# Layer 0's keys turned by a product with a diagonal matrix instead of a scaling and a transpose, and the last table load placed behind two copies

## The chip, the cores and the metric

The kernel runs on one core of a Trainium2 chip. The core has a matrix engine (TensorE, "PE" in the profile, with its weight loads listed apart as "PEld"), a vector engine (VectorE, "DVE"), an engine for functions by table (ScalarE, "ACT"), a general engine (GpSimd, "POOL") and a queue engine that issues the DMA transfers (SyncE, "SP"). Each engine works through its own list of instructions in order and waits at an instruction until what it needs is there. The metric is the device time of one execution in microseconds (us); lower is better.

## The reference

Two layers, each a cross attention and a feed-forward part with residuals. The change touches the cross attention of layer 0 alone, on 32 batches of 64 tokens of width 512:

```python
features_n = rmsnorm(features, fn_w)
Q = einsum('btd,fd->btf', text, Wq_w) + Wq_b        # text: layer norm of x
K = einsum('bsd,fd->bsf', features_n, Wk_w) + Wk_b
Q = rmsnorm(Q, qn_w)
K = rmsnorm(K, kn_w)
scores = einsum('btf,bsf->bts', Q, K) / sqrt(512)
x = x + einsum('bts,bsf->btf', softmax(scores), features_n)
...                                                 # layer 0's ffn, layer 1's attention and ffn
```

All of it is in 32-bit floats.

## The kernel before

The 2048 token rows are 16 tiles of 128 rows. Layer 0's attention goes through them in eight passes of two tiles, `for i in range(NP)` with i from 0 to 7. A pass holds four batches of 64 tokens.

In pass i, `keys_of` turns the normed tokens (`pt`, four 128x128 transposes for each tile, L181), multiplies the context by the key weights (`pk`, L374), and lets VectorE take each product out of PSUM into `kb`, one row for each key, scaled by the context's own norm and with the bias added (L377). ScalarE sums the squares of `kb` into `sq` (L381). `queries_of` makes the queries in the same way (`pq`, L397; `qb`, L398; squares, L400), turns them (`ptq`, L181) and copies them to `qT` (L405). `norm_of` turns the sums of squares into one over the root mean square, by a square root on ScalarE (L356) and a reciprocal on VectorE (L357).

The keys of pass i are turned one pass later, in pass i+1, by `turn_keys`: VectorE scales the rows of `kb` in place by `sq` (L415, one instruction for each of two tiles), TensorE transposes the scaled rows (`ptk`, eight transposes, L181 through the helper `transposed`), and VectorE takes the result out of PSUM with the norm weights multiplied in (`kT`, L420). TensorE then adds the values of the pass before (`po`, L471) and makes the scores (`psc`, L432, 16 products of 64x64). The last pass has no successor: it turns its own keys too, inside `queries_of` through `between()`.

The softmax takes the largest score (L437), multiplies it with the queries' scale (L439; in the last pass L441, which also multiplies by `one`), and takes the exponential on ScalarE (L445). ScalarE needs another table for the exponential than for the square root, and each change of table is an `ACT_TABLE_LOAD`. In the last pass a one-element exponential that gives the number 1 (`one`, L409) makes the table load happen before the scores are there; L441 reads `one`, and so waits for it.

The framework puts the instructions of every engine into an order before the kernel runs; `tc.issue_after(x)` puts what is inside behind x, and a tile from a pool waits until the buffer's last user is done. On TensorE the order of a later pass is `pt` x8, `pk` x8, `pa_t` (turned softmax weights), `ptk` x8, `po` x4, `psc` x16, `pq` x8, `ptq` x8, with some steps of layer 0's feed-forward part between them. GpSimd meanwhile makes sums of weights (L127) and products for the feed-forward part's choice (L272), which are started behind the normed context `cn` (L451). SyncE issues tokens (L314), context (L320, L325), and weights for the feed-forward part (L516, L522, L610).

One matrix product in 32-bit floats shows in the trace as two records of TensorE, a transpose as one.

Of the kernel before, what the change touches and what calls it, by code (L numbers as in the profile page):

```python
# [8 lines left out]
F32 = mybir.dt.float32  # L9
I32 = mybir.dt.int32  # L10
BF16 = mybir.dt.bfloat16
AF = mybir.ActivationFunctionType
ALU = mybir.AluOpType
# [3 lines left out]
P = 128  # L17
# [3 lines left out]
C = D // P  # L21
# [14 lines left out]
def tile_kernel(  # L36
# [25 lines left out]
    nc = tc.nc  # L62
# [5 lines left out]
    ident = const.tile([P, P], F32, name="ident")  # L68
# [110 lines left out]
    def transposed(ps, src):  # L179
        for c in range(C):  # L180
            nc.tensor.transpose(ps[:, c, :], src[:, c * P : (c + 1) * P], ident)  # L181


    with ExitStack() as l0:
# [108 lines left out]
        with ExitStack() as pa:  # L293
            wpool = pa.enter_context(tc.tile_pool(name="l0w", bufs=1))
            wk = pa.enter_context(tc.tile_pool(name="l0work", bufs=2))
# [11 lines left out]
            one = wpool.tile([P, 1], F32, name="one")  # L307
# [47 lines left out]
            def norm_of(sq):  # L355
                nc.scalar.activation(sq, sq, AF.Sqrt, bias=eps6, scale=1.0 / D)  # L356
                nc.vector.reciprocal(sq, sq)  # L357

            def keys_of(i, ct, xn, rs):

                kb = wk.tile([P, 2, D], F32, name=f"kb_{i}", tag="kb")
                sq = small.tile([P, 4], F32, name="sq4", tag="sq4")
                xT = wk.tile([P, 2, C, P], F32, name="xT", tag="xT", bufs=1)
                for tt in range(2):
                    pt = ps_t.tile([P, C, P], F32, name="pt", tag="pt")
                    transposed(pt, xn[:, tt, :])
                    turned = nc.scalar.copy(xT[:, tt], pt)
                if i == 0:
                    with tc.issue_after(turned.ins):
                        norm_context(cn[0], rs[:, 2:4])  # L370
                for tt in range(2):
                    pk = ps_m.tile([P, D], F32, name="pk", tag="pm")
                    for c in range(C):
                        nc.tensor.matmul(  # L374
                            pk, ct[:, c, tt * P : (tt + 1) * P], WK[:, c, :], start=c == 0, stop=c == C - 1
                        )
                    nc.vector.scalar_tensor_tensor(  # L377
                        kb[:, tt, :], pk, rs[:, 2 + tt : 3 + tt], bk, ALU.mult, ALU.add
                    )
                    scr = wk.tile([P, D], F32, name="scr", tag="scr", bufs=1)  # L380
                    nc.scalar.activation(scr, kb[:, tt, :], AF.Square, accum_out=sq[:, 2 + tt : 3 + tt])  # L381
                return kb, sq, xT

            def queries_of(i, xT, sq, between):

                qT = wk.tile([P, 2, C, P], F32, name=f"qT_{i}", tag="qT")
                qb = wk.tile([P, 2, D], F32, name="qb", tag="qb", bufs=1)
                last = i == NP - 1
                if last:
                    norm_of(sq[:, 2:4])  # L390

                    with tc.issue_after(exped[-1]):
                        nc.scalar.activation(one, eps6, AF.Sqrt)
                for tt in range(2):
                    pq = ps_m.tile([P, D], F32, name="pq", tag="pm")
                    for c in range(C):
                        nc.tensor.matmul(pq, xT[:, tt, c, :], WQ[:, c, :], start=c == 0, stop=c == C - 1)  # L397
                    query_added.append(nc.vector.tensor_add(qb[:, tt, :], pq, bq).ins)  # L398
                    scr = wk.tile([P, D], F32, name="scr", tag="scr", bufs=1)
                    nc.scalar.activation(scr, qb[:, tt, :], AF.Square, accum_out=sq[:, tt : tt + 1])  # L400
                between()
                for tt in range(2):
                    pt = ps_t.tile([P, C, P], F32, name="ptq", tag="pt")
                    transposed(pt, qb[:, tt, :])
                    nc.scalar.copy(qT[:, tt], pt)  # L405
                norm_of(sq[:, 0:2] if last else sq)
                if last:

                    nc.scalar.activation(one, sq[:, 0:1], AF.Exp, scale=0.0)  # L409
                return qT  # L410

            def turn_keys(kb, sq):
                kT = [wk.tile([P, C, P], F32, name="kT", tag="kT") for _ in range(2)]
                for tt in range(2):
                    nc.vector.tensor_scalar(  # L415
                        kb[:, tt, :], kb[:, tt, :], sq[:, 2 + tt : 3 + tt], None, ALU.mult
                    )
                    pt = ps_t.tile([P, C, P], F32, name="ptk", tag="pt")
                    transposed(pt, kb[:, tt, :])
                    nc.vector.tensor_mul(kT[tt], pt, wqk[:, :, None].to_broadcast([P, C, P]))  # L420
                return kT

# [168 lines left out]
            for i in range(NP):  # L591
# [27 lines left out]
                kb, sq, xT = keys_of(i, ct.pop(i), xn, rs)  # L619
                if i == 0:  # L620
                    ready = norm(1, cn[1])
                if i:
                    rs1, kb1, sq1, qT = keys.pop(i - 1)
                    add = turn_and_add(i - 2) if i > 1 else lambda: None
                    kT = turn_keys(kb1, sq1)
                    add()
                    *scored[i - 1], (_, _, normed) = scores(cn[i - 1], rs1, qT, sq1, kT)
                    with started_behind(normed):
                        sum_up()
                        for n in range(*{3: (0, 2), 4: (2, 4), 5: (4, 6), 6: (6, 7), 7: (7, 8)}.get(i, (0, 0))):  # L630
                            w = [t[:, :, QW * (n // 4) : QW * (n // 4) + QW] for t in W1]
                            four_sums(nc.gpsimd, w[4:], *w[:4], False, (n % 4,))
                place(i, 1)

                def between():
                    if i == NP - 1:
                        add = turn_and_add(i - 1)
                        last.append(turn_keys(kb, sq))
                        add()

                qT = queries_of(i, xT, sq, between)
                keys[i] = (rs, kb, sq, qT)
                place(i, 2)
# [12 lines left out]
        with ExitStack() as pb:  # L656
            wk = pb.enter_context(tc.tile_pool(name="ffnwork", bufs=2, reuse_waits="tile"))
# [180 lines left out]
    with ExitStack() as pc:  # L838
# [3 lines left out]
        wk = pc.enter_context(tc.tile_pool(name="l1work", bufs=2, reuse_waits="tile"))  # L842
# [123 lines left out]
        def project_q(xts, g, T):  # L966

            w = load_weights(q_quarter, WQS, g, T, False, "wq", 7)
            qT = wk.tile([P, 8, J, S], F32, name="qT1", tag="qT1", bufs=1)
            qsq = wk.tile([P, 8, J, S], F32, name="qsq", tag="qsq", bufs=1)  # L970

            def mm(i, ps, first):
                last = products(
                    ps, lambda h, c: w[i][:, c, h * HD : (h + 1) * HD],
                    lambda h, c: xts[RIGHT[i]][:, c, :], first,
                )
                projected.append(last.ins)
                if T == 0:
                    keep_sum(w, i, WQS, g, False, last)

            def quarter(t, hh, th):
                return t[:, 4 * th : 4 * th + 4, 2 * hh : 2 * hh + 2, :].rearrange("p b j t -> p j b t")

            def put(hh, th, ps, kept):
                o = quarter(qT, hh, th)
                ps = ps.rearrange("p j (b t) -> p j b t", t=S)
                if kept is None:
                    keeps.append(nc.scalar.copy(o, ps).ins)
                else:
                    ins = nc.vector.tensor_add(o, ps, kept.rearrange("p j (b t) -> p j b t", t=S))  # L990
                    puts.append(ins.ins)
                o = qT[:, 4 * th : 4 * th + 4, 2 * hh : 2 * hh + 2, :]
                nc.scalar.activation(  # L993
                    qsq[:, 4 * th : 4 * th + 4, 2 * hh : 2 * hh + 2, :], o, AF.Square
                )

            winograd(bank, mm, sbuf_keep, put)
            return qT, qsq
# [228 lines left out]
        qT, qsq = project_q(xts, 0, 0)  # L1227
# [12 lines left out]
        for n, (T, g) in enumerate(units):  # L1240
# [14 lines left out]
            if more:  # L1255
# [9 lines left out]
                qT, qsq = project_q(xts, g2, T2)  # L1265
# [223 lines left out]
```

## Time and profile before

| | |
|---|---|
| three runs | 1830.59, 1834.60, 1836.09 us; median 1834.6 us |
| the profiled execution | 1834.12 us, span 1832.3 us |
| granted TensorE clock | 0.997 of full speed, mean |
| busy in the span: PE, DVE, ACT, POOL | 1807.5, 945.5, 655.2, 733.7 us |
| layer 0's attention | the first 179.6 us of the span |
| in it: `ptk` transposes | 64 records on TensorE |
| in it: scaling of `kb` (L415) | 16 instructions on VectorE, 13.4 us |

A row of the groups reads: line, engine, operation, output and inputs by the program's names, shapes, count; then busy time in us and the mean of one in ns; then the engine's idle time just before and what ended it. A row of a timeline reads: start in us, us, engine, line, operation, count, and in brackets the idle time before it with what ended it. Where several equal instructions follow each other, a timeline merges them; the start of the next row is then a better end than start plus length, since TensorE's matmuls overlap at their ends. The chain of waits is followed back from the last instruction and is given here in order of time.

### The profile page before, as it was taken

The page shows a single profiled execution, that of the slowest core. Times are in us where ns is not written, and L with a number is a line of the kernel's source. Part 1 is how long each engine was busy: PE and PEld are TensorE (multiplying, and loading weights), DVE is VectorE, ACT ScalarE, POOL GpSimd, SP SyncE. Part 2 cuts the span into 40 slices and gives each one's busy share as a digit, 9 for nine tenths or more (in the row PEclk, how much of TensorE's full clock was granted, in tenths as well). Part 3 has the DMA queues.
Part 4 walks back from the last instruction along what each step waited for, and adds up shares of the span by engine and source line. Part 5 has one row for each costly group of instructions (what it writes and reads, how often), then busy time and mean ns, then how long its engine had stood idle before and what let it go on. Part 6 is the DMA issues. An engine that isn't in the chain of part 4 may idle for free.

```text
span 1832.3 us, 29495 instructions
## 1 busy us (share of the span) xinstructions
PE 1807.5 (99%) x11620; PEld 1472.1 (80%) x11620; DVE 945.5 (52%) x1665; ACT 655.2 (36%) x1187; POOL 733.7 (40%) x630
## 2 busy tenths in 40 slices
PE   8999999999999999999999999999999999999998
PEld 4545989888998888888888888888888888888764
DVE  5887555655425444445444445444444554544466
ACT  4544322222113433434343334333342434434411
POOL 1542444344337575654422344324242342222422
PEclk9999999999999999999999999999999999999999
DMA  9632300000024434544444354443454334443413
GB/s 252 183 116 89 128 22 22 21 22 22 22 69 146 148 117 157 183 158 127 137 128 128 114 150 122 130 129 112 130 154 130 118 119 132 139 133 102 160 40 93
DMA packets 157210, 210.89 MB, mean 115 GB/s; under 512 B 14928, under 2 KB 95824, under 8 KB 156432
## 3 DMA queue, kind: packets, MB, share of 16 engines
q1 hardware_dynamic: 155712, 206.91, 37.1%
q8 instruction: 92, 1.51, 0.3%
q10 hardware_dynamic: 1360, 2.10, 0.3%
q14 instruction: 46, 0.38, 0.1%
HBM read 176.74 MB, written 32.21 MB: 114 GB/s over the span
## 4 chain that ended last, share of the span: by engine, by line
PE 93%; DVE 2%; ACT 2%; POOL 1%; DMA 1%; issue 1%; SPq 0%; POOLq 0%; ACTq 0%; DVEq 0%
PE b L901 51%; PE ph L727 10%; PE po L770 9%; PE sc L1065 3%; PE pv L1124 3%; PE pq L397 3%; PE pd L1334 2%; PE pk L374 2%; PE pr L1037 2%; PE pta L1106 2%; PE pt L181 1%; PE pi L279 1%; PE ptk L1023 1%; DVE x L1413 0%; PE psc L432 0%
## 5 line engine op out<-in xcount | busy, mean ns | idle before, releaser
L1154 DVE TENSOR_TENSOR x<-x,b 128x512 f32<-128x512 f32 x224 | 153.8, 687 | 208.4 <-PE b L901 208.4
L901 PE MATMUL b<-tx,wq 128*128 128x256 f32 x1024 | 243.2, 383 | 2.8 <-POOL tx L127 1.4
L901 PE MATMUL b<-wo,so 128*128 128x256 f32 x1024 | 232.5, 380 | 3.8 <-issue 3.8
L127 POOL TENSOR_TENSOR so<-oT 128x512 f32<-128x512 f32 x64 | 81.0, 1287 | 359.1 <-ACT oT L1130 359.1
L901 PEld LDWEIGHTS b<-tx,wq 128*128 128x128 f32 x1024 | 191.0, 190 | 40.4 <-ACT keep L909 7.7
L901 PEld LDWEIGHTS b<-wo,so 128*128 128x128 f32 x1024 | 194.7, 190 | 30.9 <-issue 4.4
L901 PE MATMUL b<-xt,wq 128*128 128x256 f32 x768 | 186.2, 381 | 0.0
L901 PE MATMUL b<-wo,oT 128*128 128x256 f32 x768 | 184.9, 381 | 0.0
L1089 POOL TENSOR_TENSOR prob<-prob,mx 128x512 f32<-128x512 f32 x64 | 67.9, 1063 | 247.4 <-DVE mx L1088 129.5
L901 PEld LDWEIGHTS b<-wo,oT 128*128 128x128 f32 x768 | 145.6, 191 | 20.3 <-issue 1.0
L901 PEld LDWEIGHTS b<-xt,wq 128*128 128x128 f32 x768 | 143.1, 190 | 19.1
L1110 ACT COPY aT<-pta 128x512 f32<-128x512 f32 x64 | 34.5, 589 | 303.2 <-PE pta L1106 303.2
L909 ACT COPY keep<-b 128x512 f32<-128x512 f32 x144 | 82.4, 582 | 136.7 <-PE b L901 136.7
L901 PE MATMUL b<-wkv,sc 128*128 128x256 f32 x512 | 115.7, 379 | 0.0
L993 ACT ACTIVATE qsq<-qT 128x512 f32<-128x512 f32 x128 | 80.3, 628 | 88.9 <-DVE qT L990 88.2
L901 PEld LDWEIGHTS b<-wkv,sc 128*128 128x128 f32 x512 | 97.2, 190 | 13.2
L272 POOL TENSOR_TENSOR e<-e,down 128x896 f32<-128x896 f32 (+1 forms) x40 | 68.2, 1711 | 90.4 <-DVE e L268 88.8
L1077 DVE TENSOR_REDUCE mx<-prob 128x8 f32<-128x512 f32 x64 | 43.9, 686 | 116.7 <-POOL prob L1072 116.7
L770 PE MATMUL po<-w,gT 128*128 128x256 f32 x448 | 101.9, 382 | 0.0
L770 PEld LDWEIGHTS po<-w,gT 128*128 128x128 f32 x448 | 84.0, 190 | 18.7 <-issue 7.8
L990 DVE TENSOR_TENSOR qT<-b,keep 128x512 f32<-128x512 f32 x96 | 65.6, 686 | 57.4 <-PE b L901 57.4
L901 PE MATMUL b<-wkv,ct 128*128 128x256 f32 x384 | 94.8, 383 | 0.0
(213 smaller groups left out, 3142.4 us busy)
## 6 DMA issues: line engine op xcount, KB each, us to landing
wq<-in_wq SPq DMA_DIRECT2D x104, 256.0 KB
wo<-in_wo SPq DMA_DIRECT2D x104, 256.0 KB
wq<-wqs SPq DMA_DIRECT2D x96, 256.0 KB
wo<-wos SPq DMA_DIRECT2D x96, 256.0 KB
wkv<-in_wkv SPq DMA_DIRECT2D x52, 256.0 KB
wkv<-wks SPq DMA_DIRECT2D x48, 256.0 KB
wqs<-wq SPq DMA_DIRECT2D x32, 256.0 KB
wos<-wo SPq DMA_DIRECT2D x32, 256.0 KB
```

What stands on the lines that cost most here:

```text
L127: ins = eng.tensor_tensor(s[k], *pairs[k], op)
L272: nc.gpsimd.tensor_tensor(e3, e3, down[:, None, :].to_broadcast([P, k, BLK]), ALU.mult)
L397: nc.tensor.matmul(pq, xT[:, tt, c, :], WQ[:, c, :], start=c == 0, stop=c == C - 1)
L727: nc.tensor.matmul(ps[:, c, :], W1[LEFT[i]][:, d, (c0 + c) * P : (c0 + c + 1) * P], xq[RIGHT[i]][:, d, :], start=first and c == 0 and d == ...
L770: nc.tensor.matmul(ps, chunk(gq[LEFT[i]], c), W2[RIGHT[i]][:, c, :], start=first and c == 0, stop=c == HC - 1, skip_group_check=True,)
L901: last = nc.tensor.matmul(out[:, h, :], lhs(h, c), rhs(h, c), start=first and h == 0 and c == 0, stop=c == 1, skip_group_check=True,)
L909: keeps.append(nc.scalar.copy(e, ps).ins)
L990: ins = nc.vector.tensor_add(o, ps, kept.rearrange("p j (b t) -> p j b t", t=S))
L993: nc.scalar.activation(qsq[:, 4 * th : 4 * th + 4, 2 * hh : 2 * hh + 2, :], o, AF.Square)
L1065: score = nc.tensor.matmul(sc[k * S : (k + 1) * S, 4 * a + 2 * pp + b, :], qT[:, at, 2 * pp + k, :], kT[:, bb * S : (bb + 1) * S], start=T ...
L1089: ins = nc.gpsimd.tensor_tensor(pr, pr, mx[:, 1, :, None].to_broadcast([P, 8, S]), ALU.mult)
L1154: added.append(nc.vector.tensor_add(xq[:, i, j], xq[:, i, j], ps).ins)
```

## The change

`turn_keys` no longer scales the key rows. VectorE makes, for each tile, a 128x128 matrix `diag` that is the unit matrix with row p multiplied by the key's factor (L418 in the new file), and TensorE multiplies the unscaled rows by it: four ordinary products of 128x128 with `diag` as the moving operand in place of four transposes with the unit matrix. The result in PSUM is the same turned and scaled block. In the last pass, the one-element exponential with its table load is put behind the second copy of `qT`.

```diff
                 for tt in range(2):
                     pt = ps_t.tile([P, C, P], F32, name="ptq", tag="pt")
                     transposed(pt, qb[:, tt, :])
-                    nc.scalar.copy(qT[:, tt], pt)
+                    copied = nc.scalar.copy(qT[:, tt], pt)
                 norm_of(sq[:, 0:2] if last else sq)
                 if last:
-                    nc.scalar.activation(one, sq[:, 0:1], AF.Exp, scale=0.0)
+                    with tc.issue_after(copied.ins):
+                        nc.scalar.activation(one, sq[:, 0:1], AF.Exp, scale=0.0)
                 return qT

             def turn_keys(kb, sq):
                 kT = [wk.tile([P, C, P], F32, name="kT", tag="kT") for _ in range(2)]
                 for tt in range(2):
-                    nc.vector.tensor_scalar(
-                        kb[:, tt, :], kb[:, tt, :], sq[:, 2 + tt : 3 + tt], None, ALU.mult
-                    )
+                    diag = wk.tile([P, P], F32, name="diag", tag="diag", bufs=2)
+                    nc.vector.tensor_scalar(diag, ident, sq[:, 2 + tt : 3 + tt], None, ALU.mult)
                     pt = ps_t.tile([P, C, P], F32, name="ptk", tag="pt")
-                    transposed(pt, kb[:, tt, :])
+                    for c in range(C):
+                        nc.tensor.matmul(
+                            pt[:, c, :], kb[:, tt, c * P : (c + 1) * P], diag, start=True, stop=True
+                        )
                     nc.vector.tensor_mul(kT[tt], pt, wqk[:, :, None].to_broadcast([P, C, P]))
                 return kT
```

In the order of the instructions, TensorE's and GpSimd's lists stay as they are but for the products. On ScalarE the table load and `one` change places with the two copies. On VectorE a few neighbours change places: in pass 1 one scaling of the context (L451) comes ahead of the two `kT`, and the second normed token tile ahead of `qb`; in pass 5 one normed token tile ahead of `kb`. On SyncE, in pass 2, a token load moves ahead of the turned context, one load of the feed-forward weights (L610) ahead of the context load (L320) and four stores (L522), and another ahead of the load of L516.

## The prediction

> **What bounds it now.** I read the page first: TensorE is busy nearly all the time, and its list keeps its order under the change. A delay of TensorE in layer 0 therefore moves all that follows, and time is won only where TensorE stands idle. (PEld overlaps PE.)
>
> ```profile
> PE 1807.5 (99%) x11620; PEld 1472.1 (80%) x11620; DVE 945.5 (52%) x1665; ACT 655.2 (36%) x1187; POOL 733.7 (40%) x630
> ```
>
> Then the groups of the first 200 us, shapes apart, for the prices and for the idle time around the operations touched:
>
> ```profile
> L181 PE MATMUL ptk<-ident,kb 128*128 128x128 f32 x64 | 8.3, 273 | 0.0
> L432 PE MATMUL psc<-kT,qT 128*64 128x64 f32 x256 | 9.2, 225 | 3.6 <-DVE kT L420 2.5 <-ACT qT L405 0.9
> ...
> L415 DVE TENSOR_SCALAR kb<-kb,sq 128x512 f32<-128x512 f32 x16 | 13.4, 857 | 0.1
> L498 DVE TENSOR_SCALAR wqk<-wqk 128x4 f32<-128x4 f32 x1 | 0.2, 170 | 0.0
> ```
>
> TensorE never idles ahead of `ptk`; it idles behind it, ahead of `psc`. The scaling by VectorE costs no time by itself, only through `kT`. The listed idle time between 20 and 180 us is 1.61 + 0.91 + 0.52 + 0.89 + 0.74 + 0.35 = 5.0 us; that is all that can be won there at full clock.
>
> The chain of waits in pass 3 gives the rate of a transpose and the usual course behind it:
>
> ```profile
> 71.26 0.87 PE ptk L181 x8
> 72.13 1.02 PE po L471 x8
> 73.15 0.04 issue
> 73.19 1.15 PE psc L432 x32
> ```
>
> Eight transposes take 0.87 us, 109 ns each. An ordinary 32-bit product with the same operand shapes is `ph` of the feed-forward part, in TensorE's timeline at full clock:
>
> ```profile
> 185.51 2.84 PE L727 MATMUL ph<-xT,w 128*128 128x128 f32 x24
> 188.19 1.50 PE L727 MATMUL ph<-xT,w1s 128*128 128x128 f32 x12
> ```
>
> 24 records in 188.19 - 185.51 = 2.68 us are 111.7 ns each, and a product is two records: 223 ns.
>
> Last, two stretches of the timeline where TensorE does wait, pass 2 and the end of pass 7:
>
> ```profile
> 45.03 2.71 DVE L415 TENSOR_SCALAR kb<-kb,sq 128x512 f32<-128x512 f32 x2
> 45.09 2.37 POOL L127 TENSOR_TENSOR w1s<-w,w 128x896 f32<-128x896 f32 x1 [1.31 <-DVE sq L357]
> ...
> 48.52 3.30 DVE L451 SCALAR_TENSOR_TENSOR cn<-cn,rs,fnb 128x512 f32<-128x512 f32 x2
> 48.53 2.08 POOL L127 TENSOR_TENSOR w1s<-w1s,w 128x896 f32<-128x896 f32 x1 [1.07 <-DMA w<-in_w]
> ...
> 53.73 1.15 PE L432 MATMUL psc<-kT,qT 128*64 128x64 f32 x32 [1.61 <-DVE kT L420]
> ```
>
> ```profile
> 171.89 1.28 ACT L409 ACT_TABLE_LOAD   x1
> ...
> 173.19 0.20 ACT L409 ACTIVATE one<-sq 128x1 f32<-128x1 f32 x1
> 173.29 1.06 ACT L405 COPY qT<-ptq 128x512 f32<-128x512 f32 x2
> 173.91 1.17 PE L432 MATMUL psc<-kT,qT 128*64 128x64 f32 x32 [0.89 <-ACT qT L405]
> ...
> 175.53 0.22 DVE L441 SCALAR_TENSOR_TENSOR nm<-nm,one,sq 128x2 f32<-128x2 f32 x1
> 175.84 0.41 ACT L445 ACTIVATE s<-psc,nm,sq 128x64 f32<-128x64 f32 x1 [1.50 <-DVE nm L441]
> ```
>
> In pass 2, VectorE's second scaling ends 0.25 us after GpSimd's sum, and its first `cn` 2.1 us late: the two stop each other. At the end, the table load stands between `sq` and the copies, and `psc` waits for the copies.
>
> **The products.** Eight passes of eight: 8 x (223 - 109) ns = +0.92 us of TensorE a pass, 7.3 us in all. Off the path VectorE loses 16 scalings and gains 16 of a quarter the size. No row shows that size; the bounds are 0.17 us (L498, 4 elements) and 0.47 us (L415 unhindered, at 30.61 us). I take 0.25, by length between them. The dispute with GpSimd stays, so only what VectorE itself works is surely saved.
>
> A rule speaks against this: the Trainium skill, Perfetto Trace Analysis, section Transposes, says that a logical transpose should be a transpose and not a standard matmul, since it skips the arithmetic. TensorE: Matmul & The Clock Gate, Terms, puts the transpose mode at four times faster for FP32, which would make the eight products 3.48 us and the added TensorE time 8 x 2.61 = 20.9 us. The rows' factor is 2.05, and the sum goes by the rows.
>
> Pass by pass, as delay of `psc` against before:
>
> - Pass 1. Between `ptk` and `psc` lie 1.72 us of `pq`, which cover the two `kT` (1.26 us) and the `cn` put ahead of them (0.72 us; without that cover 2.0 us more). +0.92.
> - Pass 2. Unhindered, `psc` would have stood at 53.73 - 1.61 = 52.12; with two passes' products TensorE gets there at about 53.9. On VectorE the second sum of GpSimd, which a DMA starts and not TensorE, again holds `cn` until 50.6, then `kb` to 52.5 and `kT` (behind the second half of `ptk` at 53.0) to 53.8. So `psc` starts at about 53.83: the delay falls to 0.10, this pass gives -0.82. If GpSimd's sums move along with TensorE, it gives up to +0.9.
> - Passes 3, 4, 6, 7. `po` alone takes 1.02 us (170.91 to 171.93), yet `psc` follows it after 1.13: 0.11 us is a wait for `kT`. `ptk` ends 0.92 later, `kT` is ready at 73.72 in pass 3, `po` ends at 74.0, and `po` becomes the later one. 4 x (0.92 - 0.11) = +3.24.
> - Pass 5. `psc` at 118.55 comes 0.94 us after `po` could be done; VectorE has been busy without a break since 106.5. Both L415 there (0.86 and 1.08 us) shrink, the second by less because GpSimd's product runs beside it: 0.4 to 1.5 us saved. The products fill the gap: -0.02, up to +0.5.
> - The end. `ptk` +0.92 puts `ptq` at 172.85; its first copy starts 0.63 us later, as at 41.34 and 41.97, so 173.48, and `psc` at 174.10. The copies end at 174.57, the load takes 1.28 and `one` 0.2: 176.09. L441 waits for it and starts at 176.13, not 175.53. So the load leaves the copies' way and enters L441's: +0.60. Without the products the same move would give -0.36, since the copies could have begun 0.73 us earlier and then `one`, not `psc`, would be last. The exponential L445, `pa_t` and all of layer 1 queue behind L441's wait.
>
> On SyncE the two weight loads (448 KB each) pass the context load and four stores. At the 243 GB/s of the stretch from 40 to 60 us one of them takes 1.9 us; the context, issued at 52.20, is read first at 64.33 with no wait for a DMA. The load of L516 was waiting for the stores anyway. Nothing; without that cover 1.9 us.
>
> Sum: 0.92 - 0.82 + 3.24 - 0.02 + 0.60 = +3.9 us. The profiled execution of 1834.1 would become 1838.0; the median lies 0.5 above it, so 1838.5.
>
> **Rivals.** (a) The gaps aren't filled: VectorE stays behind GpSimd, passes 2 and 5 give +0.92 each. Then 2 x 0.92 + 3.24 + 0.92 + 0.60 = +6.6: 1841.2. For it speaks the long wait in pass 2; against it that the sum there follows a DMA. (b) The granted clock: a view of the windows has 1.00 up to 176, 0.63 from 176 to 178, 0.50 to 182, 0.66 to 184. `po` then takes 2.08 and not 1.02 us, the first 12 `ph` 2.72 and not 1.34, the next 24 3.17 and not 2.68: 2.9 us. If the drop fails to come, the sum is +1.0: 1835.6. If the longer idle ahead of `pa_t` (0.74 becomes 1.1) adds another, +6.8: 1841.4. The runs before spread over 5.5 us, so both are possible. (c) Faster: the product with `diag` costs one record, 112 ns. Then passes 3, 4, 6, 7 and pass 2 stay, pass 5 gives -0.94 and the end -0.36: -1.3, 1833.3. It would decide below 143 ns a product, where 6 x (added TensorE time of a pass) equals 1.64 us (the gap of pass 5, four waits of 0.11, the end's 0.36, less pass 2's 0.10). Against it: every ordinary 32-bit product of this trace has two records. (d) The move of the load brings nothing because L441 reads `one`: it is in my sum.
>
> **Numbers.** Forecast 0.50, (a) 0.24, (b) no drop 0.12, (b) another drop 0.07, (c) 0.05; 0.02 left for a product far dearer than two records. The range reaches from (c) past (a) and (b): 1833.0 to 1843.0. A measurement of this kernel tells 0.3%, 5.5 us, from no change: 1829.1 to 1840.1. Slower by more are (a) with 0.20 of its 0.24, the second drop with 0.06, 0.04 of the forecast's upper end and the 0.02: 0.32. Faster by more needs (c) with no drop: 0.02. Within: 0.66.
>
> **What would show it.** Right: `ptk` with 128 records at 112 ns; `psc` in passes 3, 4, 6, 7 right behind `po`; no wait, or a short one, ahead of `psc` in passes 2 and 5; L441 right behind `one`; layer 0's end 3 to 5 us later at equal clock. Wrong: `ptk` in 0.9 us; a wait for `kT` of over 1 us in pass 2; a `psc` of the last pass that starts before 173.9; another count of half-clock stretches.

## The result and the profile after

| | before | after |
|---|---|---|
| median of ten runs | 1833.47 us | 1837.6 us |
| lowest, highest | 1830.59, 1836.09 us | 1836.16, 1840.69 us |
| the profiled execution: time, span | 1834.12, 1832.3 us | 1837.26, 1835.5 us |
| mean granted clock in it | 0.997 | 0.998 |

The ratio of the times is 1.0024, with a 95% interval of 1.0015 to 1.0032: the changed kernel is 4.4 us slower (2.8 to 5.9). The medians differ by 4.1 us, which is 0.23%. From L424 on, a line of the changed file is 4 higher than the line of the same step before (`psc` L432 is L436, `po` L471 is L475, `kT` L420 is L424, L441 is L445).

The engines' line of the changed kernel's page has 64 matmul records more on TensorE, and nearly 7 us more of its busy time:

```profile
PE 1814.4 (99%) x11684; PEld 1479.5 (81%) x11684; DVE 943.2 (51%) x1665; ACT 654.8 (36%) x1187; POOL 733.2 (40%) x630
```

The groups of the first 204 us, TensorE's rows. A row's mean counts overlapping ends; for a rate, starts are compared further down.

```profile
L421 PE MATMUL ptk<-diag,kb 128*128 128x128 f32 x128 | 15.6, 275 | 0.0
...
L436 PE MATMUL psc<-kT,qT 128*64 128x64 f32 x256 | 9.2, 225 | 0.2 <-ACT qT L405 0.2
```

The turned keys are now 128 records, and the scores' idle time has gone from 3.6 to 0.2 us; the wait for `kT` has left the row. Between 20 and 183 us, all that TensorE still waits for is this (engine, line, what was waited for; us in total, times, longest us):

```profile
PE pa_t L463 <- ACT s L449: 1.1, 1, 1.1
PE pt L181 <- ACT qT L405: 0.5, 1, 0.5
PE po L475 <- ACT aT L465: 0.4, 1, 0.4
PE psc L436 <- ACT qT L405: 0.2, 1, 0.2
```

That is 2.2 us, none of it for a DMA; the kernel before waited 5.0 us in the same view. So TensorE waits less and is later all the same. TensorE's timeline in pass 3 shows a pass where nothing waits:

```profile
71.51 1.95 PE L421 MATMUL ptk<-diag,kb 128*128 128x128 f32 x16
73.39 1.09 PE L475 MATMUL po<-cn,aT 64*64 64x512 f32 x8
74.41 1.15 PE L436 MATMUL psc<-kT,qT 128*64 128x64 f32 x32
```

From `ptk` to `po` it is 73.39 - 71.51 = 1.88 us, against 0.97 in the same view of before (71.09 to 72.06), so the products add 0.91 us. And `psc` stands 1.02 us behind the start of `po`, just the time of `po`; before it stood 1.13 us behind.

In pass 2 (all engines) the 1.61 us ahead of `psc` are gone:

```profile
45.74 2.08 POOL L127 TENSOR_TENSOR w1s<-w,w 128x896 f32<-128x896 f32 x1 [0.16 <-DMA w<-in_w]
...
46.22 1.88 DVE L418 TENSOR_SCALAR diag<-ident,sq 128x128 f32<-128x128 f32 x2
...
49.06 1.42 DVE L455 SCALAR_TENSOR_TENSOR cn<-cn,rs,fnb 128x512 f32<-128x512 f32 x2
...
50.08 2.35 POOL L127 TENSOR_TENSOR w1s<-w1s,w 128x896 f32<-128x896 f32 x1 [2.26 <-DMA w<-in_w]
...
53.13 1.09 PE L475 MATMUL po<-cn,aT 64*64 64x512 f32 x8
53.23 0.69 DVE L424 TENSOR_TENSOR kT<-ptk,wqk 128x512 f32<-128x512 f32 x1 [0.20 <-PE ptk L421]
54.15 1.15 PE L436 MATMUL psc<-kT,qT 128*64 128x64 f32 x32
```

VectorE waits for TensorE here (the second `kT` for `ptk`), and `psc` follows `po`. The first of the two `diag` steps is held by GpSimd's first sum, though it is a quarter of the size; the pair ends 0.28 us behind it, as the two scalings did before. The two `cn` took 3.30 us before and take 1.42 now, because GpSimd's second sum, which waits for a DMA, began at 50.08 and not at 48.53.

At the end of the attention the table load has left the copies' way and stands ahead of L445:

```profile
177.32 1.07 ACT L405 COPY qT<-ptq 128x512 f32<-128x512 f32 x2 [1.66 <-PE ptq L181]
...
177.96 1.17 PE L436 MATMUL psc<-kT,qT 128*64 128x64 f32 x32 [0.24 <-ACT qT L405]
...
178.41 1.28 ACT L410 ACT_TABLE_LOAD   x1
...
179.70 0.20 ACT L410 ACTIVATE one<-sq 128x1 f32<-128x1 f32 x1
179.94 0.22 DVE L445 SCALAR_TENSOR_TENSOR nm<-nm,one,sq 128x2 f32<-128x2 f32 x1 [0.47 <-ACT one L410]
...
181.19 0.33 PE L463 MATMUL pa_t<-ident,s 128*128 128x128 f32 x1 [1.11 <-ACT s L449]
```

The wait ahead of `psc` is 0.24 and not 0.89 us, the one ahead of `pa_t` 1.11 and not 0.74.

The last reading is the clock. The windows view has, behind the stretch and its length, the busy time of each engine, then PEclk, DMA share and GB/s. First the kernel before, then the changed one:

```profile
176.00:177.00 1.00, 0.26 (x3) 0.18 (x1) 0.86 (x3) 0.73 (x4) 0.00 (x0) 0.77 0.45 131
177.00:178.00 1.00, 0.65 (x5) 0.39 (x8) 0.98 (x2) 0.27 (x1) 0.41 (x1) 0.50 0.58 162
...
183.00:184.00 1.00, 1.00 (x9) 1.00 (x9) 0.00 (x0) 0.07 (x1) 0.00 (x0) 0.82 1.08 444
```

```profile
181.00:182.00 1.00, 0.46 (x2) 0.27 (x4) 1.00 (x4) 0.40 (x3) 0.00 (x0) 0.97 0.88 97
182.00:183.00 1.00, 1.00 (x8) 0.30 (x8) 0.39 (x1) 0.00 (x0) 1.00 (x1) 0.50 0.55 159
...
185.00:186.00 1.00, 1.00 (x9) 1.00 (x9) 1.00 (x2) 0.00 (x0) 0.00 (x0) 0.82 1.08 370
```

All windows left out are at 0.50. Counted as time at half clock, before has 0.46 + 6 + 0.36 = 6.8 us, after has 0.06 + 3 + 0.36 = 3.4 us. So the two profiled executions do not stand on the same clock, and the spans' difference of 3.2 us has to be taken apart. The first `pt` comes 0.28 us later; from there to the last `pa_t` the changed kernel loses 4.13 us at full clock; from `pa_t` to the first `ph` it wins 0.12; and the first 36 records of `ph` take 2.12 + 2.68 us and not 2.72 + 3.17, which wins 1.09. 0.28 + 4.13 - 0.12 - 1.09 = 3.20 us, the whole of 1835.5 - 1832.3. Nothing of the difference lies behind layer 0's attention but this clock.

### The profile page after: what moved, and what is told of

The parts are those of the page before. It is cut to its first block, busy times and chain, and to the rows that moved or that the text cites. A ratio compares the mean times of both kernels' runs of the same rounds, so it can differ in the third digit from the quotient of the medians.

```text
span 1835.5 us, 29626 instructions
## 1 busy us (share of the span) xinstructions
PE 1814.4 (99%) x11684; PEld 1479.5 (81%) x11684; DVE 943.2 (51%) x1665; ACT 654.8 (36%) x1187; POOL 733.2 (40%) x630
## 4 chain that ended last, share of the span: by engine, by line
PE 95%; ACT 2%; DVE 1%; POOL 0%; issue 0%; DMA 0%; SPq 0%; POOLq 0%; ACTq 0%
PE b L905 51%; PE ph L731 10%; PE po L774 9%; PE sc L1069 4%; PE pv L1128 3%; PE pk L374 3%; PE pq L397 3%; PE pd L1338 2%; PE pr L1041 2%; PE pta L1110 2%; PE pt L181 1%; PE pi L279 1%; PE ptk L421 1%; PE ptk L1027 1%; PE po L475 1%; DVE x L1417 0%
```

## The experiments

The theory under test is the prediction's: TensorE pays two records for each product; the waits of passes 2 and 5 and four waits of 0.11 us are filled by that; the load's move costs at the end, because L441 reads `one`. The rivals are that VectorE, GpSimd or the load's place carries the loss, and that a diagonal step as such (not the product) is what costs.

The kernels ran in two groups, with a kernel before in each (1832.7 and 1832.4 us). The start of a trace differs between executions with the landing of the first transfers (the first `ptk` starts between 31.74 and 33.65 us), and the half-clock stretch comes and goes. The traces are therefore compared by the own delay of each pass: how much later than before `psc` starts, less the same for the pass ahead of it. "End" is the same for the last `pa_t`, less pass 7.

| own delay, us | pass 2 | 3 | 4 | 5 | 6 | 7 | end |
|---|---|---|---|---|---|---|---|
| after, predicted | -0.82 | +0.81 | +0.81 | -0.02 | +0.81 | +0.81 | +0.60 |
| after, measured | -0.76 | +0.80 | +0.95 | 0.00 | +0.80 | +0.81 | +0.63 |
| products alone | -0.77 | +0.81 | +1.15 | +0.12 | +0.80 | +0.81 | +0.26 |
| load alone | -0.83 | -0.01 | +0.11 | +0.35 | -0.01 | +0.01 | -0.29 |
| transposes with diagonal | -0.46 | 0.00 | +0.30 | -0.04 | 0.00 | 0.00 | -0.28 |
| products twice | +1.02 | +2.59 | +2.50 | +1.86 | +2.59 | +2.60 | +2.41 |
| scaling on ScalarE | -0.68 | 0.00 | +0.30 | -0.93 | -0.01 | +0.01 | -0.29 |
| no scaling | -1.58 | +1.10 | -0.19 | -0.94 | 0.00 | 0.00 | 0.00 |
| matrix on ScalarE | -0.77 | +0.81 | +0.78 | -0.13 | +0.81 | +0.81 | +0.62 |
| ScalarE, no wait for `one` | -1.57 | +0.62 | -0.17 | -0.94 | 0.00 | 0.00 | -0.74 |

**The products alone.** The changed kernel with the load at its old place:

```diff
-                    with tc.issue_after(copied.ins):
-                        nc.scalar.activation(one, sq[:, 0:1], AF.Exp, scale=0.0)
+                    nc.scalar.activation(one, sq[:, 0:1], AF.Exp, scale=0.0)
```

> The products with the diagonal matrix as in the changed kernel; the last table load again ahead of the two copies, as before. My theory (TensorE's added time less the gaps it fills, and a last wait of L441 for the load): up to the last pass everything as in the changed kernel; in the last pass the load (over by about 1.5 us after the square root) no longer stands in the copies' way because the products have put the turned queries later, so the largest-score step follows the scores at once and the last turned weights pa_t start about 0.4 us earlier than in the changed kernel. 3.7 us above before, 0.4 below the changed kernel. Rival (the move of the load is the useful half and hides part of the products): 0.4 us or more above the changed kernel.

Measured: 1836.0 us, ratio 1.0025 (1.0015 to 1.0035), not told apart from the whole change by time. The trace tells them apart; ScalarE and VectorE at the end:

```profile
177.60 1.28 ACT L409 ACT_TABLE_LOAD   x1
...
179.25 1.07 ACT L405 COPY qT<-ptq 128x512 f32<-128x512 f32 x2 [0.15 <-PE ptq L181]
...
181.10 0.29 DVE L440 TENSOR_REDUCE nm<-psc 128x2 f32<-128x128 f32 x1 [0.42 <-PE psc L435]
181.50 0.22 DVE L444 SCALAR_TENSOR_TENSOR nm<-nm,one,sq 128x2 f32<-128x2 f32 x1
```

With the products, TensorE reaches `ptq` only when the load is done: the copies wait 0.15 us for TensorE and not for the load. The end costs 0.26 and not 0.63, so the load's move loses 0.37 us beside the products. The small differences in passes 4 and 5 are a late `xn` (0.33 us of idle time).

**The load alone.** The kernel before with the load behind the copies:

```diff
-                    nc.scalar.copy(qT[:, tt], pt)
+                    copied = nc.scalar.copy(qT[:, tt], pt)
...
-                    nc.scalar.activation(one, sq[:, 0:1], AF.Exp, scale=0.0)
+                    with tc.issue_after(copied.ins):
+                        nc.scalar.activation(one, sq[:, 0:1], AF.Exp, scale=0.0)
```

> Scaling and transposes as before; only the last table load moved behind the two copies. My theory: psc of the last pass starts about 0.7 us earlier, then L441 waits for the load, and the exponential is about 0.36 us earlier than before; the time 0.4 us below before, which the times can't tell from none. Rival (the load behind the copies is always late): the exponential later than before by 0.3 us or more.

Measured: 1832.1 us, ratio 0.9999 (0.999 to 1.0007). The timeline of the end:

```profile
172.34 1.17 PE L433 MATMUL psc<-kT,qT 128*64 128x64 f32 x32 [0.24 <-ACT qT L405]
172.80 1.28 ACT L410 ACT_TABLE_LOAD   x1
...
174.33 0.22 DVE L442 SCALAR_TENSOR_TENSOR nm<-nm,one,sq 128x2 f32<-128x2 f32 x1 [0.47 <-ACT one L410]
```

Against pass 7, `psc` comes 0.66 us earlier and `pa_t` 0.29: more than half of the gain at the copies is taken back by the wait for `one`. The same edit wins 0.29 us without the products and loses 0.37 with them. Pass 2 changed here too (-0.83), although the instructions ahead of it are the same and in the same order on every compute engine; the gap ahead of `psc` was 0.78 and not 1.61. So its size varies between executions. Passes 4 and 5 gave 0.46 us of it back, 0.3 of that ahead of `pk` in pass 5, in a stretch for which the profile lists no cause. A fraction of a microsecond may not be read from the passes up to 5 of one execution.

**One record for each product.** The kernel before with the load moved, a `diag` made by the same kind of step at the same place, and transposes in place of products:

```diff
-                    nc.vector.tensor_scalar(
-                        kb[:, tt, :], kb[:, tt, :], sq[:, 2 + tt : 3 + tt], None, ALU.mult
-                    )
+                    diag = wk.tile([P, P], F32, name="diag", tag="diag", bufs=2)
+                    nc.vector.tensor_scalar(diag, ident, sq[:, 2 + tt : 3 + tt], 0.0, ALU.mult, ALU.is_gt)
...
-                    transposed(pt, kb[:, tt, :])
+                    for c in range(C):
+                        nc.tensor.transpose(pt[:, c, :], kb[:, tt, c * P : (c + 1) * P], diag)
```

> The changed kernel with the products replaced by transposes that use the same freshly made 128x128 matrix, its diagonal set to 1 (the keys' factor is left out). All dependencies, the smaller VectorE step and the moved load stay; only TensorE's price goes. My theory: the 4 us turn round; psc of passes 3, 4, 6, 7 without an own delay, passes 2 and 5 win 0 to 1.6 and 0.4 to 0.9, the end 0.36: 1.2 to 2.9 us below before. Rival (the time lies in the new wait for the matrix or in the changed order of VectorE and SyncE): at least 2 us above before.

Measured: 1832.77 us, ratio 1.0002 (0.9993 to 1.0011). The loss of the change is gone with the second record. One thing besides the record changed, against the expectation: VectorE and SyncE have the order of the kernel before here (the `cn` of pass 1 behind the two `kT`, the load of L610 behind the context load), as in every kernel that keeps the transposes. This kernel alone therefore doesn't separate the record from that order. The change's own trace does: its TensorE waits for no DMA and for no `kT`, and passes 3, 6 and 7 lose what the records cost.

The gain that was expected on top did not come: from pass 2 on it is 0.48 us. Pass 2 kept a wait of 1.15 us for `kT`. Pass 5 kept one too, and VectorE's timeline says why; first the kernel before, then this one.

```profile
106.91 0.72 POOL L127 TENSOR_TENSOR w2t<-w2p,w2t 128x256 f32<-128x256 f32 x1
107.06 0.86 DVE L415 TENSOR_SCALAR kb<-kb,sq 128x512 f32<-128x512 f32 x1
...
111.24 2.22 POOL L272 TENSOR_TENSOR e<-e,down 128x448 f32<-128x448 f32 x2 [0.55 <-DVE e L268]
...
112.67 1.08 DVE L415 TENSOR_SCALAR kb<-kb,sq 128x512 f32<-128x512 f32 x1
```

```profile
107.49 1.14 POOL L272 TENSOR_TENSOR e<-e,down 128x448 f32<-128x448 f32 x1
107.68 1.02 DVE L418 TENSOR_SCALAR diag<-ident,sq 128x128 f32<-128x128 f32 x1
...
112.03 2.22 POOL L272 TENSOR_TENSOR e<-e,down 128x448 f32<-128x448 f32 x2 [1.57 <-DVE e L268]
...
113.45 0.88 DVE L418 TENSOR_SCALAR diag<-ident,sq 128x128 f32<-128x128 f32 x1
...
119.13 1.15 PE L434 MATMUL psc<-kT,qT 128*64 128x64 f32 x32 [0.70 <-DVE kT L422]
```

Both `diag` steps start beside a product of GpSimd and end 0.07 and 0.08 us behind it, at 108.70 and 114.33. The two full scalings started beside GpSimd as well and ended 0.29 us behind it, at 107.92 and 113.75. So a held step gains some 0.2 us by being a quarter of the size, and the length of the wait depends on where in GpSimd's instruction it starts: the `diag` steps take 1.90 us together, where the scalings took 1.94, and 0.70 us of the gap stays.

**The products twice.**

```diff
-                        nc.tensor.matmul(
-                            pt[:, c, :], kb[:, tt, c * P : (c + 1) * P], diag, start=True, stop=True
-                        )
+                        for _ in range(2):
+                            nc.tensor.matmul(
+                                pt[:, c, :], kb[:, tt, c * P : (c + 1) * P], diag, start=True, stop=True
+                            )
```

> The changed kernel with every product made twice into the same place. My theory: the gaps that could be filled are filled already, so each of the 64 added products costs its two records of 112 ns in full: 14.3 us above the changed kernel, about 1852. Rival (TensorE still has room in these passes): under 10 us. If a product were a single record's worth in effect: 7 us.

Measured: 1850.56 us, ratio 1.0104 (1.0089 to 1.012), which is 0.0080 or 14.7 us above that of the change (13.7 by the medians, each less that of its kernel before). In passes 3, 6, 7 and at the end each own delay is 1.78 or 1.79 us above the change's: 16 records of 112 ns. TensorE's and VectorE's timelines in pass 2 give both prices unhindered:

```profile
47.40 0.48 DVE L418 TENSOR_SCALAR diag<-ident,sq 128x128 f32<-128x128 f32 x2
...
52.43 3.74 PE L422 MATMUL ptk<-diag,kb 128*128 128x128 f32 x32
...
56.10 1.09 PE L476 MATMUL po<-cn,aT 64*64 64x512 f32 x8
```

32 records fill 56.10 - 52.43 = 3.67 us, and a `diag` step that GpSimd leaves alone takes 0.24 us. With TensorE this late nothing waits for `kT`, and products add to the time one for one.

**The scaling taken from VectorE.** The kernel before with the load moved and the rows scaled by ScalarE:

```diff
-                    nc.vector.tensor_scalar(
-                        kb[:, tt, :], kb[:, tt, :], sq[:, 2 + tt : 3 + tt], None, ALU.mult
-                    )
+                    nc.scalar.activation(
+                        kb[:, tt, :], kb[:, tt, :], AF.Copy, scale=sq[:, 2 + tt : 3 + tt]
+                    )
```

> Transposes as before, the key rows scaled by ScalarE (a copy with a factor for each row) and not by VectorE, the last table load behind the copies. My theory: TensorE's price is gone, and the scaling no longer stands in VectorE's list behind GpSimd: pass 5 wins its 0.9 us, pass 2 0.8 to 1.6, the end 0.3; 2.0 to 2.8 us below before. Rival (the gaps of passes 2 and 5 are set by GpSimd's sums and the DMA, not by the scaling): the end's 0.3 alone. A second rival (ScalarE's 0.6 us for each tile falls on the way from the norms to the scores): passes lose up to 0.6 each, time above before.

Measured: 1831.35 us, ratio 0.9993 (0.9984 to 1.0001): 1.3 us below before, less than expected and not told from none. Pass 5 gives its gap back whole (-0.93, no wait left). Pass 2 does not; the timeline there:

```profile
47.95 3.25 DVE L452 SCALAR_TENSOR_TENSOR cn<-cn,rs,fnb 128x512 f32<-128x512 f32 x2
48.44 2.21 POOL L127 TENSOR_TENSOR w1s<-w1s,w 128x896 f32<-128x896 f32 x1 [1.00 <-DMA w<-in_w]
...
53.12 1.15 PE L433 MATMUL psc<-kT,qT 128*64 128x64 f32 x32 [0.93 <-DVE kT L421]
```

GpSimd's second sum came in the midst of the two `cn`, so 0.93 us stayed. The profiled execution had two half-clock stretches of 6.8 us, and its time of 1833.33 lies above the median.

**No scaling at all.** The three lines of L415 taken out of the kernel before; the load stays where it was.

> The kernel before without the scaling of the key rows (left out of the computation); transposes and the table load as before. It bounds from above what any relief of VectorE can be worth. My theory: only passes 2 and 5 have a wait that VectorE sets; 0.9 us in pass 5, 0.8 to 1.6 in pass 2, nothing elsewhere: 1.7 to 2.5 us below before. Rival (the gaps are set elsewhere): each under 0.3.

Measured: 1830.3 us, ratio 0.9987 (0.9978 to 0.9996): 2.4 us (0.7 to 4.0). This bounds what VectorE's part was worth. Passes 2 and 5 give 1.58 and 0.94 us and have no wait left, the end gives nothing. But pass 3 takes 1.10 us back, so that the trace wins 1.61 us from pass 2 on: VectorE waited 1.11 us for a square root that ScalarE made late, behind a table load, and reached `qb` only after three `xn`, and TensorE waited 0.72 us for `qb`. In pass 2 the sum came late here:

```profile
50.18 1.41 DVE L448 SCALAR_TENSOR_TENSOR cn<-cn,rs,fnb 128x512 f32<-128x512 f32 x2
51.94 2.09 POOL L127 TENSOR_TENSOR w1s<-w1s,w 128x896 f32<-128x896 f32 x1 [2.43 <-DMA w<-in_w]
```

**The matrix from ScalarE.** The changed kernel with `diag` made by another engine:

```diff
-                    nc.vector.tensor_scalar(diag, ident, sq[:, 2 + tt : 3 + tt], None, ALU.mult)
+                    nc.scalar.activation(diag, ident, AF.Copy, scale=sq[:, 2 + tt : 3 + tt])
```

> The changed kernel with its diagonal matrix made by ScalarE instead of VectorE. My theory: with the products TensorE has no gap left that VectorE sets, so nothing is won: every psc of passes 3 to 7 within 0.15 us of the changed kernel, the time as the changed kernel's. Rival (VectorE, held by GpSimd, still carries part of the 4 us): passes 2 to 5 together at least 0.5 us earlier than in the changed kernel.

Measured: 1838.03 us, ratio 1.0026 (1.0016 to 1.0036), as with the change. Counted from pass 2 to pass 5 it is 0.30 us earlier than the change: less than the rival's 0.5, though 0.17 of it in pass 4 is just more than the 0.15 allowed for. ScalarE makes the two matrices of pass 5 in 0.69 us, where VectorE took 1.81, and VectorE is free of its 8.8 us in all; the loss is still there. So it is not VectorE's step that costs.

**A version that beats both.** The scaling on ScalarE and the load behind the copies, as above, and the last pass without `one`:

```diff
-            *scored[NP - 1], (product, most, _) = scores(cn[NP - 1], rs, qT, sq, last[0], one)
+            *scored[NP - 1], (product, most, _) = scores(cn[NP - 1], rs, qT, sq, last[0])
```

> As the kernel with the scaling on ScalarE and the load behind the copies, and the largest-score step no longer reads the number 1 of the one-element exponential, so that VectorE doesn't wait for the load; the exponential of the scores follows it in ScalarE's list anyway. My theory: the wait of L441 for the load (0.47 us in the load-only kernel) goes, pa_t of the last pass 0.4 to 0.5 us earlier; 2.4 to 3.3 us below before. Rival (ScalarE itself is late, and the exponential starts no earlier): 0.1 or less.

Measured: 1829.77 us, ratio 0.9986 (0.9977 to 0.9995), 2.6 us below the kernel before. The end of the attention:

```profile
171.07 1.28 ACT L410 ACT_TABLE_LOAD   x1
171.84 0.29 DVE L438 TENSOR_REDUCE nm<-psc 128x2 f32<-128x128 f32 x1 [0.42 <-PE psc L433]
172.17 0.16 DVE L440 TENSOR_TENSOR nm<-nm,sq 128x2 f32<-128x2 f32 x1
172.37 0.20 ACT L410 ACTIVATE one<-sq 128x1 f32<-128x1 f32 x1
172.48 0.39 ACT L446 ACTIVATE s<-psc,nm,sq 128x64 f32<-128x64 f32 x1
```

`nm` no longer waits for `one`; the exponential starts right behind the load, and the end gives 0.74 and not 0.29 us (pass 2 gives 1.57 here, of which pass 3 takes 0.62 back). That is the part of the load's move that the wait on `one` had eaten: 0.45 us.

## Why the prediction was right

The forecast of 1838.5 us was for the likeliest case, and that case came. The median is 0.9 us lower for a reason that has nothing to do with the change: the three runs of before had a median of 1834.6, ten have 1833.47, 1.1 us less. The medians of ten differ by 4.1 us, the sum said 3.9.

- **The products.** Right. 128 records at 112 ns; the price was taken from `ph`, an ordinary product of the same shape. The loss is shown to be TensorE's records: with one record the loss is gone, with the products doubled it grows by 14.7 us, and with the matrix from another engine it stays. What the changed order on VectorE and SyncE might cost was not run by itself; the change's trace shows no wait that would come from it, and pass 1 loses 0.90 us for a predicted 0.92. The rule in the Trainium skill (Perfetto Trace Analysis, Transposes) speaks in the right direction, and the trace puts 223 against 109 ns to it.
- **Passes 3, 4, 6, 7.** Right: +0.80, +0.95, +0.80, +0.81 for a predicted +0.81. The four waits of 0.11 us for `kT`, too short to show as idle time, were there and were filled. Pass 4 has 0.14 us more, from an `xn` held on VectorE ahead of the third `pt`; the matrix from ScalarE takes that away.
- **Pass 2.** The size came right (-0.76 for -0.82) by luck; the step behind it was wrong. The prediction had `psc` set by VectorE at 53.83, behind GpSimd's second sum. By its own numbers TensorE, at about 53.9, was the later of the two and should have set it. `psc` came at 53.87 (54.15 less the late start of 0.28), set by TensorE. The sum, which was to stay where it was, began 1.55 us later than before, and TensorE's `pa_t` 1.19 us later. Both bounds lay within 0.1 us of each other, so the error cost nothing. The bound by VectorE was not tested: in no trace with the products did the sum hold the two `cn` for as long as before (2.37 us at most, against 3.30). The kernels with scaling on ScalarE show how the sum meets the `cn` to be chance: in one it fell on both and left a wait of 0.93 us, in the other it came when they were almost done. (The second scaling before ended 0.28 us behind the first sum, and not the 0.25 that the prediction read.)
- **Pass 5.** The delay was right (0.00 for -0.02). The term for VectorE was mis-sized: 0.4 to 1.5 us of saving were forecast, and the two steps went from 1.94 to 0.92 + 0.89 = 1.81 us. The gap was closed by the products coming later, not by VectorE being earlier.
- **The price of `diag`.** Mis-sized in the mean, and right for a step that nothing holds. It was put at 0.25 us; the view of the tile gives, in ns, the least, the median and the greatest:

```profile
L418 DVE TENSOR_SCALAR diag<-ident,sq x16: 266/304/1683, 30.9 to 165.5; 128x128 f32<-128x128 f32 x16
```

The mean is 569 ns, 8.8 us in all against 13.4 of L415. A `diag` step that starts beside one of GpSimd's instructions ends just behind it, as in pass 5 above. The Trainium skill (SBUF — State Buffer, Who interferes with whom) says that VectorE in a two-port mode and GpSimd lock each other out for the whole instruction; the pair in pass 2 (1.88 us where two unhindered take 0.48) and the two of pass 5 (0.92 and 0.89 us) agree. The loss is off the path here, since TensorE became the later one.

- **The end.** Right: +0.63 for +0.60, and the sign turned with the products as forecast (-0.29 measured for -0.36 without, +0.37 with).
- **The rivals.** (a) did not come: the gaps of passes 2 and 5 were filled. (b) came in half: the drop stayed, but for 3.4 and not 6.8 us, which was worth 1.09 us in the profiled execution. (c) was tried as such, with one record: its -1.3 us lies at the edge of the interval (-1.3 to +2.0 us against before), the trace from pass 2 on has -0.48, and its term of 0.94 us for pass 5 fails, because `diag` is held.
- **The signs named ahead.** All came: 128 records at 112 ns, `psc` right behind `po`, no wait ahead of `psc` in passes 2 and 5, L441 (now L445) right behind `one`, and an end of the attention 4.13 us later at equal clock. Of the signs against it, one was half there: as many half-clock stretches, but the first a shorter one.

Left open: why the half-clock stretch at the end of layer 0 has one length in one execution and twice that in the next. No run changed it on purpose.

## What to carry to other kernels

A step that can be folded into a matrix product is free only if the product was there already: here a transpose of one record became a product of two, on the engine that was busy for 99% of the span. Price such an exchange by an ordinary product of the same shape in the same trace, then go pass by pass and see which idle time the longer work fills. Making a step smaller brought little where another engine held it; moved to a third engine (ScalarE here) it gave back the whole wait of pass 5, and a dummy step that only forces a table load is best not read by the path.

## What the runs showed of the hardware

- The half-clock stretches have fixed lengths. In the ten traces they come, while TensorE has work, at the end of layer 0 and again between 1763 and 1791 us, each for 3.4 or 6.8 us, and in two kernels the first was missing. The spread of one kernel goes with them: for the changed kernel, 1840.69 us had a mean clock of 0.996, 1836.58 us one of 0.999. The Trainium skill (TensorE: Matmul & The Clock Gate, What's actually happening) names a free-running window of about 3.4 us; the stretches are one or two of these. In the changed kernel little idle time came with the drop: waits of 0.24, 1.11 and 0.36 us over some 4 us, with thin products between them. And idle time alone does not decide: without the scaling, waits of 0.89, 0.74 and 0.35 us at the same place brought no drop.
- The start differs between executions with the landing of the first transfers. With the products alone VectorE waited 1.35 us for tokens up to 22.55 us, and TensorE then 1.09 us for `qb`; the kernel before had neither wait. The first `ptk` starts 1.9 us apart in the ten traces. The gap of pass 2 was 1.61 us in one trace and 0.78 in another, with the same code ahead of it.
